# The last seven steps of a packed graph convolution in another order, and a ninth gathered tile fetched by rows

## The chip, the cores and the metric

The kernel runs on one core of a Trainium2 chip. Its time is the device time of one execution in microseconds (us); lower is better. The engines of the core are TensorE (PE in the profile), VectorE (DVE), ScalarE (ACT), GpSimd (POOL) and SyncE (SP). Each has a program of its own that it works off in order; they wait for one another through semaphores.

## The reference

One layer of a message-passing network over 12500 nodes of 128 features and 400000 edges that are sorted by destination:

```python
rbf = jnp.exp(-(distances[:, None] - centers) ** 2 / (2.0 * width * width))      # 50 centres
cut = 0.5 * (jnp.cos(jnp.pi * distances / CUTOFF) + 1.0) * (distances <= CUTOFF)
W = (jax.nn.silu(rbf @ fw1 + fb1) @ fw2 + fb2) * cut[:, None]
messages = (h[src] @ pw + pb) * W
agg = jax.ops.segment_sum(messages, dst, num_segments=num_atoms)
h2 = h + (jax.nn.silu(agg @ mw1 + mb1) @ mw2 + mb2)
x = _layernorm(x + h2, axis=-1, eps=1e-05)
```

The lengths are drawn from 0 to some 56 and the cutoff is 10, so under a fifth of the edges has a weight other than zero.

## The kernel before

**Tiles.** The kernel packs the edges that are within the cutoff into a dense list while it runs, in seven chunks, and works on the list in tiles of 512 edges (4 groups of 128; `QE = QT * P`). For this input 139 tiles are used (`NL = 139`, numbered `q` = 0 to 138). `proj`, the product h @ pw + pb of all nodes, is first computed and written to memory; a tile then fetches the 512 rows of `proj` that its edges' sources name.

**One tile.** `fetch(q)` lets GpSimd issue one indirect DMA for each group of 128 rows: four for a tile, in order of `q` (line 1088). Two tiles at a time (`o`, an "oct"), `basis` has ScalarE compute the radial basis by a Square and an Exp (lines 1140 and 1144), `first` multiplies it on TensorE (line 1156), and `silu` applies Silu on ScalarE (line 1162). For one tile, `second` multiplies by the second weight matrix into a bank of PSUM (lines 1171 and 1174), `message` multiplies that bank by the gathered rows on VectorE (line 1189), `place` makes the 0/1 matrix of destinations times the cutoff weight on VectorE (line 1201), `sum_up` sums the messages by destination with four matmuls for each window (line 1221), and `add` adds the sums to the table `aggT` on VectorE, at a base read from the packed list (line 1255).

**Tiles fetched by rows.** In twelve tiles the first group of 128 rows isn't gathered by GpSimd. For the eight of `BY_SP` SyncE issues 128 DMAs of one row (512 bytes) each (`one_row`, line 1064), for the four of `BY_ACT` ScalarE does. SyncE reads the row numbers into registers, 32 at a time (line 1060), and writes into one of three buffers in turn. How many rows go into a step is set by a clock that the program keeps while it is written out: `one_by_one` puts rows until `row_at` has passed the clock, and each row counts `A_ROW` = 0.58. The multiplication of that group waits for all 128 rows of the tile (line 1186).

**Nodes.** When all edges up to a node are summed, blocks of nodes are finished: `node_first` (line 1268, then Silu on ScalarE into `zs`, line 1270), `node_second` (line 350), `node_stats` (the residual sum, line 1305, and the layernorm's statistics, line 1309), `deviations` (small VectorE operations, lines 1316 to 1319, then a Sqrt on ScalarE, line 1325), `scales` (lines 1335 and 1336), `normalize` (line 1356 on ScalarE or 1353 on VectorE) and a store from SyncE (line 193). The first 80 blocks of 128 nodes go four at a time, and their deviations sixteen blocks at a time (16 columns); the last are named in `TAIL`: 80 and 84 of four blocks, 88, 90, 92, 94 and 96 of two. ScalarE loads another table whenever it goes from Exp to Silu, to Sqrt and back (ACT_TABLE_LOAD in the profile).

**What sets the order.** All of it stands in the program as it is written. A loop over `q` in `range(NL - 7)` has the steps of tiles 0 to 131; the last seven steps (132 to 138) and the end are written out one by one, since each has other node blocks beside it. Each engine takes its instructions in this order, so what stands ahead on an engine delays what stands behind it. SyncE's queue holds loads of `x`, stores of the output and the row DMAs in one order; a store there waits until ScalarE has normalized its block. In addition, the gathers of tiles below `UPTO` = 90 depend on a VectorE instruction some places back (`BACK`, `behind`, `logged`, and the dependence added in `fetch`). `keep_busy(n)` issues n matmuls whose results nobody reads.

Of the kernel before, what the change touches and what calls it, by code (L numbers as in the profile page):

```python
# [43 lines left out]
NL = 139  # L44
# [16 lines left out]
BACK = ((0, 66), (16, 38), (26, 46), (39, 38), (52, 26), (63, 19), (88, 46), (102, 14),  # L61
        (111, 8))
UPTO = 90
VECTORS = ("TensorScalarPtr", "TensorTensor", "CopyPredicated", "TensorReduce", "TensorCopy",
           "BNStats")
# [28 lines left out]
def kernel(  # L94
# [346 lines left out]

    vectors = []

    def logged(i):

        if i.engine == mybir.EngineType.DVE and str(i.opcode) in VECTORS:
            vectors.append(i.name)

    nc.push_inst_callback(logged)

    def behind(q):

        return next(n for at, n in reversed(BACK) if q >= at)

# [627 lines left out]
    def fetch(q, idx=None, table=None, js=range(QT)):  # L1082
        got = quad_sb[place_of(q) if q >= 0 else 0]
        for j in js:
# [3 lines left out]
            g = nc.gpsimd.indirect_dma_start(  # L1088
                out=got[:, j, :], out_offset=None, in_=proj if table is None else table,
                in_offset=bass.IndirectOffsetOnAxis(ap=i, axis=0))  # L1090
# [312 lines left out]
    def nodes(q):  # L1403
# [6 lines left out]
        for k, t0 in enumerate(early):  # L1410
            if begin[t0][0] - 5 == q:
                load_x(t0)
            if begin[t0][2] == q:
# [3 lines left out]
                if k % 4 == 3:  # L1417
# [9 lines left out]
    st_of, deep = {}, []  # L1427

    def tail(q):

        for k, t0, step in ((9, 80, node_first), (8, 80, node_second), (8, 84, node_first)):
# [142 lines left out]
    for q in range(NL - 7):  # L1574
# [72 lines left out]
    assert not todo and counted and not ready and len(deep) == 1 and done[0] == NL - 7  # L1647
# [12 lines left out]
    st = statistics()  # L1660
    node_stats(80, st)
# [16 lines left out]
    sum_up(q, message(q))  # L1678
    second(q + 2)
    node_second(88)  # L1680
    place(q + 1)
    add(q)
    normal(1)
# [183 lines left out]
```

## Time and profile before

| | |
|---|---|
| runs | 720.64, 720.64 and 723.32 us, median 720.64 us |
| profiled execution | 718.53 us, of which the span is 717.0 us |
| granted TensorE clock, mean | 0.918 |
| GpSimd indirect DMAs | 551, from 6.78 to 701.36 us of the span |
| busy share of the span | TensorE 82%, VectorE 78%, GpSimd 74%, ScalarE 56% |
| last matmul of `sum_up` | starts at 707.73 us |
| end of the last normalization on VectorE | 713.24 us |

All times in the profile count from the start of the span; the execution is 1.5 us longer than it. A row of the timeline gives the start, the duration, the engine, the line, the operation, what it writes and reads, and in brackets how long the engine had been idle before it and what ended the idle time. Busy shares are means over 717 us and over stages with different limits; they don't say which engine the others wait for.

### The profile page before, as it was taken

The page shows a single profiled execution, that of the slowest core. Times are in us where ns is not written, and L with a number is a line of the kernel's source. Part 1 is how long each engine was busy: PE and PEld are TensorE (multiplying, and loading weights), DVE is VectorE, ACT ScalarE, POOL GpSimd, SP SyncE. Part 2 cuts the span into 40 slices and gives each one's busy share as a digit, 9 for nine tenths or more (in the row PEclk, how much of TensorE's full clock was granted, in tenths as well). Part 3 has the DMA queues.
Part 4 walks back from the last instruction along what each step waited for, and adds up shares of the span by engine and source line. Part 5 has one row for each costly group of instructions (what it writes and reads, how often), then busy time and mean ns, then how long its engine had stood idle before and what let it go on. Part 6 is the DMA issues. An engine that isn't in the chain of part 4 may idle for free.

```text
span 717.0 us, 14503 instructions
## 1 busy us (share of the span) xinstructions
PE 584.6 (82%) x3526; PEld 461.1 (64%) x3526; DVE 561.7 (78%) x1741; ACT 401.7 (56%) x569; POOL 529.2 (74%) x565
## 2 busy tenths in 40 slices
PE   5878868688898788697878997799998887878775
PEld 5767557566676576575666765577686654665554
DVE  8899899759998799989979994876856545555765
ACT  6557625245645667554645566466765843574564
POOL 6777777777777777777777777777777777777771
PEclk9998787899999899889987999699999998999997
DMA  8996533333334333443344334444543444344242
GB/s 259 328 328 206 161 99 102 98 102 84 115 103 130 83 87 100 118 126 85 87 113 118 99 116 116 130 131 120 153 113 91 138 111 114 101 142 126 56 131 79
DMA packets 54004, 91.41 MB, mean 127 GB/s; under 512 B 14272, under 2 KB 21536, under 8 KB 53914
## 3 DMA queue, kind: packets, MB, share of 16 engines
q0 software_dynamic: 17712, 36.51, 20.4%
q1 hardware_dynamic: 24916, 35.61, 15.0%
q10 hardware_dynamic: 11286, 18.31, 8.0%
q8 instruction: 29, 0.48, 0.3%
q14 instruction: 61, 0.50, 0.2%
HBM read 74.59 MB, written 15.79 MB: 126 GB/s over the span
## 4 chain that ended last, share of the span: by engine, by line
POOL 18%; DVE 15%; DMA 13%; issue 13%; PE 9%; ACT 3%; ACTq 3%; DVEq 1%; SPq 0%; POOLq 0%
POOL quad L1088 14%; DMA quad<-proj,srci 8%; POOL x L1088 3%; DVE hot L1201 3%; PE ph L1156 3%; DMA x<-proj,srci 3%; DVE msg L1189 2%; ACTq L1064 2%; PE sums L1221 2%; PE bank L1174 1%; DVE aggT L1255 1%; DMA packed<-line,at_i 1%; DVE quad L1189 1%; DMA pair<-packed 1%; DVE quad L1201 1%
## 5 line engine op out<-in xcount | busy, mean ns | idle before, releaser
L1088 POOL DMA_INDIRECT quad<-proj,srci x402 | 381.7, 950 | 122.6 <-issue 97.3
L1174 PEld LDWEIGHTS bank<-fw_sb,s 128*128 128x128 f32 x1112 | 158.1, 205 | 60.3 <-issue 50.2
L1174 PE MATMUL bank<-fw_sb,s 128*128 128x128 f32 x1112 | 158.2, 289 | 0.0
L1156 PE MATMUL ph<-rbf,w_sb 102*128 102x512 f32 x278 | 143.7, 642 | 12.3 <-ACT s L1162 8.3
L1221 PEld LDWEIGHTS sums<-hot,msg 128*128 128x128 f32 x816 | 109.2, 200 | 53.4 <-issue 26.0
L1162 ACT ACTIVATE s<-ph 128x1024 f32<-128x1024 f32 x70 | 71.2, 1017 | 122.3 <-PE ph L1156 121.9
L1201 DVE TENSOR_SCALAR hot<-iota_n,dl,cut 128x80 f32<-128x80 f32 (+4 forms) x408 | 111.1, 347 | 22.9 <-PE sums L1221 20.9
L1221 PE MATMUL sums<-hot,msg 128*128 128x80 f32 (+4 forms) x816 | 111.5, 282 | 15.4 <-DVE msg L1189 15.2
L1088 POOL DMA_INDIRECT x<-proj,srci x94 | 90.0, 958 | 28.7 <-issue 22.3
L1171 PE MATMUL bank<-fb_b,ones_b 96*128 96x512 bf16 x139 | 56.0, 403 | 42.2 <-DVE msg L1189 22.0
L1189 DVE TENSOR_TENSOR msg<-bank,quad 128x512 f32<-128x512 f32 (+1 forms) x78 | 52.5, 673 | 41.1 <-DMA quad<-proj,srci 34.5
L1156 PEld LDWEIGHTS ph<-rbf,w_sb 102*128 102x128 f32 x278 | 51.2, 205 | 51.7 <-issue 37.3
L1255 DVE TENSOR_TENSOR aggT<-aggT,sums 128x80 f32 (+4 forms) x209 | 54.1, 259 | 30.7 <-PE sums L1221 12.4
L1140 ACT ACTIVATE rbf<-d_sb,rbf_bias,rbf_scale 102x512 f32<-102x512 f32 x70 | 56.2, 803 | 8.0 <-issue 8.0
L1088 POOL DMA_INDIRECT quad<-in_x_dram,srci x48 | 47.5, 990 | 15.9 <-issue 12.5
L1162 ACT ACT_TABLE_LOAD x34 | 43.6, 1283 | 15.3 <-issue 14.9
L1144 ACT ACT_TABLE_LOAD x35 | 44.9, 1283 | 11.4 <-issue 9.6
L1221 PE MATMUL sums<-quad,quad 128*128 128x128 f32 (+3 forms) x296 | 41.8, 285 | 11.0 <-DVE quad L1189 11.0
L350 PEld LDWEIGHTS bank<-pw_sb,xT 128*128 128x128 f32 (+1 forms) x292 | 42.3, 209 | 11.2 <-issue 5.6
L1144 ACT ACTIVATE rbf<-rbf 102x512 f32<-102x512 f32 x70 | 44.1, 630 | 7.9 <-issue 5.6
L1221 PEld LDWEIGHTS sums<-quad,quad 128*128 128x128 f32 x296 | 38.6, 201 | 12.7 <-DVE quad L1189 12.4
L350 PE MATMUL bank<-pw_sb,xT 128*128 128x128 f32 (+1 forms) x292 | 42.8, 293 | 0.8 <-ACT xT L995 0.6
(281 smaller groups left out, 796.9 us busy)
## 6 DMA issues: line engine op xcount, KB each, us to landing
d_sb<-near_d ACTq DMA_DIRECT2D x67, 256.0 KB
row_sb<-proj SPq DMA_DIRECT2D x1024, 0.5 KB
x<-in_x_dram SPq DMA_DIRECT2D x46, 256.0 KB
row_sb<-proj ACTq DMA_DIRECT2D x512, 0.5 KB
quad<-proj,srci POOLq DMA_INDIRECT x402
proj<-hp SPq DMA_DIRECT2D x24, 256.0 KB
out_dram<-x SPq DMA_DIRECT2D x22, 256.0 KB
x<-proj,srci POOLq DMA_INDIRECT x94
```

Of the source, the lines that this page charges most:

```text
L350: nc.tensor.matmul(to[:m, k, :], lT[:, k * P:k * P + m], w, start=False, stop=(k == a + c - 1))
L1088: g = nc.gpsimd.indirect_dma_start(out=got[:, j, :], out_offset=None, in_=proj if table is None else table, in_offset=bass.IndirectOffsetO ...
L1140: a = nc.scalar.activation(rbf[:u], d[:u], AF.Square, bias=rbf_bias[:u], scale=rbf_scale[:u])
L1144: nc.scalar.activation(rbf[:u], rbf[:u], AF.Exp, scale=-1.0 / (2.0 * width * width))
L1156: nc.tensor.matmul(ph[:, h, :], w1_sb[:2 * KR, h, :], rbf[:2 * KR], start=True, stop=True)
L1162: nc.scalar.activation(s[:, :n], ph[:, :n], AF.Silu)
L1171: nc.tensor.matmul(pu, ones_b[:, :P], bias_b["fb2"].rearrange("k j f -> k (j f)"), start=True, stop=False)
L1174: nc.tensor.matmul(pu[:, j * H:(j + 1) * H], s[:, j * P:(j + 1) * P], fw2_sb, start=False, stop=(j == QT - 1))
L1189: nc.vector.tensor_mul(msg[:, a:b, :], pu_of[q].rearrange("p (j f) -> p j f", j=QT)[:, a:b, :], got_of[q][:, a:b, :])
L1201: nc.vector.tensor_scalar(hot[:, j, :wide(q)], iota_n[:, :wide(q)], dl[:, at[0], at[1]], cut[:, at[0], at[1]], op0=OP.is_equal, op1=OP.mult)
L1221: nc.tensor.matmul(pa[:, k * W:k * W + wide(q)], msg[:, j, :], hot[:, j, :wide(q)], start=(j % n == 0), stop=(j % n == n - 1))
L1255: nc.vector.tensor_add(to, to, pa[:, k * W:k * W + wide(q)])
```

## The change

**The gathers.** `BACK`, `UPTO`, `VECTORS`, `logged`, `behind` and the dependence that `fetch` added are gone, so no gather of a tile depends any longer on a place in VectorE's program. Those dependences that the data need stay.

**The rows.** `BY_SP` has nine tiles in place of eight: 118 and 133 are replaced by 113, 124 and 135. GpSimd issues 550 indirect DMAs in place of 551, SyncE 128 row DMAs and four register loads more. Once no chunk is left to be packed (`todo` is empty), a row counts `A_ROW_LATE` = 0.42 in place of 0.58, so more rows stand in a step. On SyncE's queue the part from the store of block 60 to the store of block 64 was, before (`row_sb` is the buffer of rows; `x_87` holds block 64, the other `x_` blocks after it):

```order
L193 DMA out_dram<-x_86 128x512
L1064 DMA row_sb<-proj 1x512 x9
L193 DMA x_91<-in_x_dram 128x512
L1064 DMA row_sb<-proj 1x512 x9
L193 DMA x_92<-in_x_dram 128x512
L1064 DMA row_sb<-proj 1x512 x9
L193 DMA x_93<-in_x_dram 128x256
L1064 DMA row_sb<-proj 1x512 x2
L193 DMA x_86<-in_x_dram 128x256
L193 DMA out_dram<-x_87 128x512
```

The same part of SyncE's queue now, and one row group further:

```order
L189 DMA out_dram<-x_86 128x512
L1047 DMA row_sb<-proj 1x512 x12
L189 DMA x_91<-in_x_dram 128x512
L1047 DMA row_sb<-proj 1x512 x12
L189 DMA x_92<-in_x_dram 128x512
L1047 DMA row_sb<-proj 1x512 x4
L1043 TENSOR_LOAD at_row
L1047 DMA row_sb<-proj 1x512 x8
L189 DMA x_93<-in_x_dram 128x256
L1047 DMA row_sb<-proj 1x512 x13
L189 DMA out_dram<-x_87 128x512
L189 DMA x_86<-in_x_dram 128x256
L1047 DMA row_sb<-proj 1x512 x11
```

Twelve rows stand in a step where nine stood, and the last eleven rows (of tile 135) stand behind the store of block 64, where before all rows of tile 133 stood ahead of it.

**The node blocks.** The statistics of block 76 move from the loop to `tail(NL - 9)`, and the deviations of 64, 68 and 72 are computed without it, earlier, in the loop; so `scales`, the normalizations and the stores of these three blocks come earlier too, two of them ahead of the last octs' bases. Block 76 goes into the group of 80, 84, 88 and 90 (16 columns in place of 12). The two last octs' `basis` moves from step 131 to step 132, and their `first` and `silu` to the steps 133 and 134. On ScalarE the twelve instructions from the Silu of tiles 134 and 135 on were, before (`s` is the Silu of an oct, `zs` of a node block, `dev` the Sqrt, `rbf` a basis):

```order
L1162 ACTIVATE s<-ph 128x1024
L1270 ACTIVATE zs<-bank_170 128x512
L1325 ACT_TABLE_LOAD
L1325 ACTIVATE dev<-v,eps 128x16
L1140 ACTIVATE rbf<-d_sb,rbf_bias,rbf_scale 102x512
L1144 ACT_TABLE_LOAD
L1144 ACTIVATE rbf<-rbf 102x512
L1140 ACTIVATE rbf<-d_sb,rbf_bias,rbf_scale 102x512
L1144 ACTIVATE rbf<-rbf 102x512
L1270 ACT_TABLE_LOAD
L1270 ACTIVATE zs<-bank_168 128x512
L1162 ACTIVATE s<-ph 128x1024
```

On ScalarE now, from the Silu of that same oct:

```order
L1141 ACTIVATE s<-ph 128x1024
L1335 ACTIVATE x_87<-x_87,by,rs 128x128 x4
L1249 ACTIVATE zs<-bank_170 128x512
L1335 ACTIVATE x_88<-x_88,by,rs 128x128 x4
L1249 ACTIVATE zs<-bank_169 128x512
L1119 ACTIVATE rbf<-d_sb,rbf_bias,rbf_scale 102x512
L1123 ACT_TABLE_LOAD
L1123 ACTIVATE rbf<-rbf 102x512
L1119 ACTIVATE rbf<-d_sb,rbf_bias,rbf_scale 102x512
L1123 ACTIVATE rbf<-rbf 102x512
L1335 ACTIVATE x_89<-x_89,by,rs 128x128 x4
L1141 ACT_TABLE_LOAD
```

The Sqrt with its table no longer stands between two Silus of node blocks here, and both these Silus come ahead of the bases.

**The last steps.** In each of them `second(q + 2)` now stands ahead of `sum_up(q)`, node work is in other places, and `keep_busy` has 3 + 2 + 2 matmuls in place of 1 + 1. On TensorE the steps of tiles 136 and 137 were, before (`hot_1075,msg_1080` is the sum of tile 136, `hot_1192,msg_680` that of 137, line 1174 the `second` of tile 138, line 1288 the residual of block 96, line 1268 `node_first` of block 92):

```order
L1221 MATMUL sums<-hot_1075,msg_1080 128x128 x4
L1171 LDWEIGHTS ones_b
L1171 MATMUL bank_169<-fb_b,ones_b 128x512
L1174 MATMUL bank_169<-fw_sb,s 128x128 x4
L1285 LDWEIGHTS ones_b
L1285 MATMUL bank_167<-mb_b,ones_b 128x256
L1288 MATMUL bank_167<-x_89,ident 128x128 x2
L1288 MATMUL bank_167<-x_89,ident 84x128 x2
L1267 LDWEIGHTS mb_b
L1267 MATMUL bank_170<-ones_b,mb_b 128x256
L1268 MATMUL bank_170<-aggT,mw_sb 128x256
L1221 MATMUL sums<-hot_1192,msg_680 128x128 x4
```

On TensorE now, from the `second` of tile 138 to the `node_first` of block 92:

```order
L1153 MATMUL bank_170<-fw_sb,s 128x128 x4
L1264 LDWEIGHTS ones_b
L1264 MATMUL bank_168<-mb_b,ones_b 128x256
L1267 MATMUL bank_168<-x_89,ident 128x128 x2
L1267 MATMUL bank_168<-x_89,ident 84x128 x2
L1200 MATMUL sums<-hot_1075,msg_1080 128x128 x4
L1246 LDWEIGHTS mb_b
L1246 MATMUL bank_167<-ones_b,mb_b 128x256
L1247 MATMUL bank_167<-aggT,mw_sb 128x256
```

The `second` of tile 138 and the residual of block 96 stood behind the sum of tile 136 and stand ahead of it now; what remains between the sums of 136 and 137 is the node work of block 92 and the three `keep_busy` matmuls. The diff:

```diff
-BACK = ((0, 66), (16, 38), (26, 46), (39, 38), (52, 26), (63, 19), (88, 46), (102, 14),
-        (111, 8))
-UPTO = 90
...
-BY_SP = (22, 45, 62, 67, 86, 102, 118, 133)
+BY_SP = (22, 45, 62, 67, 86, 102, 113, 124, 135)
...
+A_ROW_LATE = 0.42
...
     def one_by_one():
         row_at[0] = max(row_at[0], clock[0] - 8.0)
         while singles[0] and row_at[0] < clock[0]:
-            row_at[0] += A_ROW
+            row_at[0] += A_ROW if todo else A_ROW_LATE
             one_row(0)
...
-            g = nc.gpsimd.indirect_dma_start(
+            nc.gpsimd.indirect_dma_start(
                 out=got[:, j, :], out_offset=None, in_=proj if table is None else table,
                 in_offset=bass.IndirectOffsetOnAxis(ap=i, axis=0))
-            if 0 <= q < UPTO and len(vectors) > behind(q):
-                tc.add_manual_dep(
-                    g.ins, vectors[-1 - behind(q)],
-                    mybir.DependencyInfo(mybir.DependencyClass.Sync, mybir.DependencyReason.DATA))
...
-            if begin[t0][2] == q:
+            if begin[t0][2] == q and t0 != early[-1]:
                 if k % 4 == 0:
                     st_of[0] = statistics()
                 node_stats(t0, st_of[0][:, k % 4 * 4:])
-                if k % 4 == 3:
+                if k % 4 == 3 or t0 == early[-2]:
                     deep.append(deviations(early[k // 4 * 4:k + 1], st_of[0]))
...
     def tail(q):
+        if q == NL - 9:
+            last_st.append(statistics())
+            node_stats(early[-1], last_st[0])
...
             for o in (q // 4 * 2 + 4, q // 4 * 2 + 5):
-                if 2 * o < NL:
+                if 2 * o < NL and q < NL - 8:
                     basis(o)
...
     q = NL - 7
     house(q)
-    sum_up(q, message(q))
+    msg = message(q)
     second(q + 2)
+    sum_up(q, msg)
+    node_second(84)
+    node_stats(80, last_st[:, 4:])
     bases_of(list(range(q, NL)))
     place(q + 1)
-    scales(*deep.pop(0))
+    for o in (octs(q), octs(q + 1)):
+        basis(o)
     add(q)
-    first(octs(q))
-    silu(octs(q))
-    node_second(84)
     normal(1)
-    st = statistics()
-    node_stats(80, st)
...
     q += 1
     house(q)
-    sum_up(q, message(q))
+    msg = message(q)
     second(q + 2)
-    first(octs(q))
-    silu(octs(q))
-    normal(1)
+    first(octs(q - 1))
+    silu(octs(q - 1))
+    sum_up(q, msg)
     place(q + 1)
+    node_stats(84, last_st[:, 8:])
     add(q)
     node_first(88)
-    node_stats(84, st[:, 4:])
...
-    dev = deviations([80, 84, 88, 90], st)
+    dev = deviations([76, 80, 84, 88, 90], last_st)
...
     p, q = NL - 2, NL - 1
     house(p)
-    sum_up(p, message(p))
+    msg = message(p)
     node_second(92)
+    keep_busy(3)
+    sum_up(p, msg)
+    node_stats(92, st)
     sum_up(q, message(q, (0, 1)), (0,))
     add(p)
     node_first(94)
+    sum_up(q, message(q, (1, 2)), (1,))
     normal(1)
-    sum_up(q, message(q, (1, 2)), (1,))
-    node_stats(92, st)
     add(q, (0,))
+    keep_busy(2)
     sum_up(q, message(q, (2, 3)), (2,))
-    normal(2)
+    normalize(*ready.pop(0), on=(0, 1))
+    store()
+    normal(1)
     node_second(94)
-    keep_busy(1)
     sum_up(q, message(q, (3, 4)), (3,))
     add(q, (1,))
     node_first(96)
     node_stats(94, st[:, 2:])
+    keep_busy(2)
     dev = variances([92, 94], st)
-    keep_busy(1)
```

More of the change, by code (lines that the diff above doesn't have):

```diff
@@ L440, in before_it @@
         return max((m for m in range(q) if place_of(m) == place_of(q)), default=-1)
[L442 to L453, printed above, removed]
     def room(q):
@@ L1425, in nodes @@
                 load_x(t0)
-    st_of, deep = {}, []
+    st_of, deep, last_st = {}, [], []
     def tail(q):
+        if q == NL - 9:
+            last_st.append(statistics())
+            node_stats(early[-1], last_st[0])
         for k, t0, step in ((9, 80, node_first), (8, 80, node_second), (8, 84, node_first)):
@@ L1677 @@
     house(q)
-    sum_up(q, message(q))
+    msg = message(q)
     second(q + 2)
+    first(octs(q - 1))
+    silu(octs(q - 1))
+    sum_up(q, msg)
     node_second(88)
@@ L1682 @@
     add(q)
-    normal(1)
     node_first(90)
-    node_stats(88, st[:, 8:])
+    node_stats(88, last_st[:, 12:])
     load_x(94)
-    normal(1)
     q += 1
     house(q)
-    sum_up(q, message(q))
+    msg = message(q)
     second(q + 2)
     node_second(90)
+    sum_up(q, msg)
     place(q + 1)
+    node_stats(90, last_st[:, 14:])
+    dev = deviations([76, 80, 84, 88, 90], last_st)
+    silu_next()
     add(q)
     load_x(96)
-    node_stats(90, st[:, 10:])
-    dev = deviations([80, 84, 88, 90], st)
-    silu_next()
     q += 1
     house(q)
-    sum_up(q, message(q))
+    msg = message(q)
     second(q + 2)
+    node_x(96)
+    sum_up(q, msg)
     place(q + 1)
-    node_x(96)
     st = statistics()
+    scales(*dev)
     add(q)
     node_first(92)
-    scales(*dev)
-    normal(1)
+    normal(2)
     place(q + 2)
@@ L1753 @@
     store()
-    nc.remove_inst_callback(logged)
     def more(q):
```

5 lines of the change are left out of this document (2 added, 3 removed).

## The prediction

> **What bounds the kernel now.** I read GpSimd's waits first, then its timeline's ends:
>
> ```profile
> span 717.0 us, 14503 instructions
> POOL quad L1088 <- issue: 109.8, 360, 0.3
> POOL quad L1088 <- DVE aggT L1255: 2.4, 8, 0.3
> POOL quad L1088 <- DVE hot L1201: 1.5, 5, 0.3
> 6.78 1.21 POOL L1088 DMA_INDIRECT quad<-in_x_dram,srci  x1 [1.60 <-DVE srci L566]
> 691.68 0.94 POOL L1088 DMA_INDIRECT quad<-proj,srci  x1 [0.30 <-DVE x L1305]
> 692.93 0.96 POOL L1088 DMA_INDIRECT quad<-proj,srci  x1 [0.30 <-issue]
> 699.18 0.94 POOL L1088 DMA_INDIRECT quad<-proj,srci  x1 [0.30 <-issue]
> 700.42 0.94 POOL L1088 DMA_INDIRECT quad<-proj,srci  x1 [0.30 <-issue]
> ```
>
> The waits' columns are total, count and longest. GpSimd's pauses are 0.3 us whether the profile finds a releaser or not, so none is a wait: a gather starts each 1.24 to 1.25 us (699.18 to 700.42), from 6.78 to 700.42 us. GpSimd's stream of gathers sets the time up to there. The rest is what follows the last gather: 717.0 − 700.42 = 16.6 us. The chain of waits gives what a gather needs to land (its start, its length; eight such rows between 600 and 685 us lie between these two), and VectorE's and TensorE's timelines show who uses the data:
>
> ```profile
> 644.16 2.45 DMA quad<-proj,srci
> 652.90 4.10 DMA quad<-proj,srci
> 667.90 2.50 DMA quad<-proj,srci
> 670.53 0.69 DVE L1189 TENSOR_TENSOR quad<-bank,quad 128x512 f32<-128x512 f32 x1 [0.85 <-DMA quad<-proj,srci]
> 697.34 0.69 DVE L1189 TENSOR_TENSOR msg<-bank,quad 128x512 f32<-128x512 f32 x1
> 706.29 0.48 DVE L1189 TENSOR_TENSOR quad<-bank,quad 128x128 f32<-128x128 f32 x2
> 706.63 0.49 PE L1221 MATMUL sums<-quad,quad 128*128 128x128 f32 x2 [0.58 <-DVE quad L1189]
> 707.73 0.38 PE L1221 MATMUL sums<-quad,quad 128*128 128x128 f32 x2
> 712.65 0.59 DVE L1353 TENSOR_SCALAR x<-x,rs,by 128x128 f32<-128x128 f32 x2
> ```
>
> At 670.53 a message still waits for its data. The last gather (700.42) should land by 702.9 at 2.50, but its message is in the pair at 706.29, so some 3.6 us late: at the very end the gathers don't bound, the chain of compute behind them does. Where it fell behind is seen on ScalarE and TensorE, and in the windows of TensorE's clock:
>
> ```profile
> 664.85 1.02 ACT L1162 ACTIVATE s<-ph 128x1024 f32<-128x1024 f32 x1 [3.78 <-PE ph L1156]
> 670.89 0.60 ACT L1270 ACTIVATE zs<-bank 128x512 f32<-128x512 f32 x1 [5.03 <-PE bank L1268]
> 671.51 1.28 ACT L1325 ACT_TABLE_LOAD   x1
> 679.07 0.60 ACT L1270 ACTIVATE zs<-bank 128x512 f32<-128x512 f32 x1
> 679.72 0.38 PE L1171 MATMUL bank<-fb_b,ones_b 96*128 96x512 bf16 x1 [2.32 <-ACT zs L1270]
> 698.09 1.31 PE L1221 MATMUL sums<-hot,msg 128*128 128x128 f32 x8 [2.39 <-DVE msg L1189]
> 689.38 1.05 PE L1174 MATMUL bank<-fw_sb,s 128*128 128x128 f32 x8
> 699.62 1.92 PE L1174 MATMUL bank<-fw_sb,s 128*128 128x128 f32 x8
> 692.13:695.54 3.41, 2.67 (x22) 2.58 (x22) 2.38 (x7) 2.65 (x5) 2.50 (x4) 1.00 0.69 212
> 695.54:698.95 3.41, 1.02 (x9) 0.87 (x8) 3.08 (x12) 1.59 (x2) 2.72 (x3) 1.00 0.36 92
> 698.95:702.37 3.42, 3.42 (x17) 3.21 (x16) 2.97 (x12) 0.20 (x1) 1.88 (x2) 0.50 0.23 56
> ```
>
> (A window's columns: length, then busy time of TensorE, its weight loads, VectorE, ScalarE and GpSimd, then the granted clock.) Between 671.51 and 679.07 ScalarE loads tables, takes the Sqrt and computes two bases ahead of a `zs` for which TensorE waits 2.32 us. Later TensorE idles 2.39 us for the message of tile 136, its window 695.54 to 698.95 has 1.02 us of work, and in the next one the clock is 0.50: the `second` of tile 138 takes 1.92 us in place of 1.05. The sums of 137 and 138 stand behind that.
>
> **The change part by part.**
>
> *One gather fewer.* One interval of 1.25 us less, since nothing else holds GpSimd: the last gather starts at 699.17. The bounds are 0 and 1.25; I take 1.25, because every interval quoted has that length. −1.25.
>
> *No dependence on VectorE.* GpSimd never waited for it (longest pause 0.3), so 0; the cover is that the gathers are issued late in any case, and GpSimd still waits for the buffers that the data need. What would be late without that cover is only an earlier gather, which would gain.
>
> *The ninth row tile.* SyncE's own price:
>
> ```profile
> L1060 SPq TENSOR_LOAD <-at_row x32: 2120/2164/3061, 76.7 to 643.9; - x32
> 562.97 5.75 SPq L1064 DMA_DIRECT2D row_sb<-proj  x18
> L1064 SPq DMA_DIRECT2D row_sb<-proj x128: 227/228/350, 521.7 to 586.6; - x128
> 606.86 0.28 DVE L1186 TENSOR_TENSOR quad<-bank,row_sb 128x128 f32<-128x128 f32 x1
> ```
>
> A row costs 5.75 / 18 = 0.32 us, a load of 32 registers 2.16, so a tile 128 × 0.32 + 4 × 2.16 = 49.6 us of SyncE at least. Before, the 128 rows of tile 118 took 64.9 us (521.7 to 586.6), at nine in a step; at twelve in a step that is 64.9 × 9/12 = 48.7, under SyncE's own 49.6. With the loads and stores between I take 52 us a tile: tile 113 done at 521.7 + 52 = 573.7, 124 at 625.7, 135 at 677.7. Needed: tile 118's rows were multiplied at 606.86; five tiles earlier at 20 gathers × 1.25, and one gather less, is 580.6 for 113; eleven tiles on, at 43 gathers, 634.4 for 124; 42 more, 686.9 for 135 (a tile by ScalarE lies between). So each is 7 to 9 us early, and the 1152 rows and the extra register loads cost 0. The eleven last rows now stand behind the store of block 64, which waits for its normalization behind the Silu that is at 664.85: about 664.85 + 1.02 + 1.6, then 11 × 0.32, some 671 us. No one waits there.
>
> *The node blocks and bases.* The Sqrt of 64 to 72 and the table loads around it (2 × 1.28 + 0.31) move ahead of a Silu at which ScalarE had been idle 3.78 and 5.03 us: covered there, 0 on the path. Gone is the stretch of 7.6 us in which it stood ahead of two `zs`. The one thing later is the `first` and `silu` of the last octs, by one step of 5 us: tile 136's Silu now ends one step ahead of its `second`, in place of two. Its own work (two matmul pairs and a Silu of 1.02) fits into a step, so 0, at least while the bases start on time.
>
> *The last steps.* Their rows on TensorE, and ScalarE's last normalizations:
>
> ```profile
> 701.54 1.45 PE L1288 MATMUL bank<-x,ident 128*128 128x128 f32 x8
> 706.95 0.27 PE L347 MATMUL bank<-mb_b,ones_b 96*128 96x256 bf16 x1
> 707.07 0.61 PE L350 MATMUL bank<-mw_sb,zs 128*128 128x128 f32 x4
> 707.51 0.38 PE L1439 MATMUL ph<-mb_b,ones_b 96*128 96x512 bf16 x1
> 706.20 3.17 ACT L1356 ACTIVATE x<-x,by,rs 128x128 f32<-128x128 f32 x8
> ```
>
> `second` of tile 138 and the residual of block 96 come ahead of the sum of 136, in the very gap of 2.39 us. They cost 1.05 + 0.38 and, of the residual's 1.45 at half clock, some 1 us of TensorE there, hidden by the wait for the message; and the window that had 1.02 us of work then has about 3, so I expect no 0.50 after it. The five more `keep_busy` matmuls are 0.38 us each in waits. If the messages wait for nothing but data, the end is: landing 2.50; 0.34 from the last message to its sum (706.29 to 706.63); and from the last sum to VectorE's end 713.24 − 707.73 = 5.51. That is 8.35 us from the last gather's start, against 713.24 − 700.42 = 12.82 before. At the slowest landing, 4.10, it is 9.95. Between the last two sums TensorE still has the `second` of block 94. It takes 0.73 us (706.95 to 707.68), and its `zs` stands on ScalarE behind normalizations; I put 0.45 of it on the path, so 8.8 us, nearer to the lower end because the row of 2.50 is the last one of this stage. That is −4.0. The 3.76 us from VectorE's end to the span's end are stores and stay. A gain beyond is possible: eight normalizations (3.17 us, to 709.37) stood directly ahead of the last Silu and now a part of them is on VectorE; worth 0.3 at most, left out of the sum.
>
> [...]
>
> *Sum.* 717.0 − 1.25 − 4.0 = 711.7 for the span. The profiled execution was 718.53, 1.5 over its span and 2.1 under the runs' median of 720.64; I take the same difference of −5.3 off the median: 715.4.
>
> **The rivals.** About 0.5%, 3.6 us, is what a measurement of this kernel can tell from no change.
>
> *A: only the gather counts.* `second(q + 2)` ahead of each sum costs TensorE 0.38 + 1.05 with overlaps, about 1.1 us, in each step. If the message is there first, the sum and everything behind waits that long, and the lag of 3.6 us stays. For it: the message of 136 at 697.34 wasn't waiting for data. Against it: TensorE idled 2.39 us right then. 720.64 − 1.25 = 719.4.
>
> *B: the rows come late (slower).* If SyncE's pace doesn't rise as the order has it, tile 135's multiplication waits, and with it VectorE and every sum behind it. It decides from (686.9 − 521.7) / 3 = 55.1 us a tile on; at 58 tile 135 is done at 695.7, 8.8 us late, against the 5.3 gained: 724.1. For it: 64.9 us before, and a queue in which stores wait:
>
> ```profile
> SPq L193 <- ACT x L1356: 84.8, 14, 26.6
> ```
>
> One such wait of 26.6 us ahead of a row tile would be enough. Against it: the stores of the blocks concerned come earlier.
>
> *C: the clock falls again.* Another window in the last 20 us with too little TensorE work. At half clock a full window loses up to 1.7 us (half of 3.42); I take 1.5: 716.9. Against it: seven `keep_busy` matmuls and the `second` in the gap.
>
> [...]
>
> **How the numbers follow.** Forecast 0.65, A 0.15, B 0.06, C 0.12, D 0.02. The forecast's own range is 714.4 to 717.0: landing up to 4.10 adds 1.6, the normalizations on VectorE take off 0.3, and 0.7 are for TensorE's queue. The whole range reaches down to 712.8, if the median falls on the profiled execution (718.53 − 5.3 = 713.2), and up to 718.9, which holds C and a third of A. Faster by over 0.5% (under 717.0) is the forecast but 0.02 and half of C, 0.69; the same is A, the rest of C and those 0.02, 0.23; slower is B and D, 0.08.
>
> **What would show it.** Right: 550 gathers with pauses of 0.3, the last at about 699.2; VectorE's multiplications of row tiles 113, 124 and 135 without a wait; the messages of tiles 134 to 138 waiting for the gather's DMA rather than for TensorE; no window at clock 0.50 after 688; VectorE's last normalization some 8.8 us behind the last gather. Wrong: an idle of VectorE ahead of a row multiplication (B), messages of 138 again over 3 us behind their data (A), a `second` of 1.9 us (C), gathers over 1.3 us apart (D).

## The result and the profile after

The changed kernel takes 715.74 us (median of 6 runs, 713.59 to 716.95), the kernel before 721.4 us (6 runs beside it, 720.64 to 723.32). The ratio is 0.9919 with a 95% interval of 0.99 to 0.9938, so 5.8 us less, between 4.5 and 7.2. The forecast was 715.4 us in a range of 712.8 to 718.9. The span of the profiled execution fell from 717.0 to 712.1 us.

GpSimd's waits and its last gathers in the changed kernel:

```profile
span 712.1 us, 14771 instructions
POOL quad L1071 <- issue: 108.6, 356, 0.3
692.23 0.94 POOL L1071 DMA_INDIRECT quad<-proj,srci  x1 [0.30 <-DVE x L1284]
699.73 0.95 POOL L1071 DMA_INDIRECT quad<-proj,srci  x1 [0.30 <-issue]
```

Ahead of a gather behind the first one no pause is over 0.3 us, and the last of 550 indirect DMAs (seven of them write the packed list) starts at 699.73, which is 0.69 us earlier than the last of 551 before. What VectorE and TensorE do with the last tiles (line 1168 is the message, 1165 its part that uses rows, 1200 the sums, 1332 a normalization; the row at 684.03 belongs to tile 134, whose rows ScalarE fetches):

```profile
680.40 0.69 DVE L1168 TENSOR_TENSOR msg<-bank,quad 128x512 f32<-128x512 f32 x1 [1.12 <-DMA quad<-proj,srci]
684.03 0.28 DVE L1165 TENSOR_TENSOR quad<-bank,row_sb 128x128 f32<-128x128 f32 x1
689.32 0.29 DVE L1165 TENSOR_TENSOR quad<-bank,row_sb 128x128 f32<-128x128 f32 x1
693.52 0.68 DVE L1168 TENSOR_TENSOR msg<-bank,quad 128x512 f32<-128x512 f32 x1
702.34 0.29 DVE L1168 TENSOR_TENSOR quad<-bank,quad 128x128 f32<-128x128 f32 x1
707.72 0.59 DVE L1332 TENSOR_SCALAR x<-x,rs,by 128x128 f32<-128x128 f32 x2
692.38 1.05 PE L1153 MATMUL bank<-fw_sb,s 128*128 128x128 f32 x8
694.27 1.16 PE L1200 MATMUL sums<-hot,msg 128*128 128x128 f32 x8
702.83 0.39 PE L1200 MATMUL sums<-quad,quad 128*128 128x128 f32 x2
```

The message of tile 136 comes at 693.52 (697.34 before). TensorE doesn't idle ahead of its sum, which follows the `second` of tile 138 at 1.05 us (1.92 before). The last message is at 702.34, 2.6 us after the start of its gather. The prediction had named one sign of being right that isn't here: no message from tile 134 on has a wait for the gather's DMA in its row. The last such wait is that of tile 133 (680.40). VectorE ends at 708.31: 8.58 us behind the last gather, where it was 12.82. From there to the span's end it is 3.79 us (3.76 before). So of the 4.9 us by which the two profiled spans differ, 0.69 are the gathers and 4.24 the last steps. TensorE's windows follow, with the columns of the prediction. In this trace the granted clock falls sixteen times, from 45.89 to 708.08, at times that are whole multiples of 3.413 us apart, and these lie elsewhere in this execution than in that of the kernel before; the windows are counted back from its fall at 708.08, behind the last matmul:

```profile
694.43:697.84 3.41, 2.16 (x16) 1.57 (x16) 3.34 (x14) 1.25 (x5) 2.50 (x3) 1.00 0.20 56
697.84:701.25 3.41, 3.05 (x23) 2.42 (x22) 2.00 (x8) 2.70 (x8) 2.23 (x3) 1.00 0.36 118
701.25:704.67 3.42, 2.97 (x18) 1.62 (x15) 2.58 (x12) 3.04 (x8) 0.00 (x0) 1.00 0.51 172
```

No window is at clock 0.50 from 688 up to the last sum. On ScalarE the two Silus of node blocks now stand ahead of the bases, as the order showed:

```profile
670.82 0.60 ACT L1249 ACTIVATE zs<-bank 128x512 f32<-128x512 f32 x1 [2.78 <-PE bank L1247]
675.22 0.60 ACT L1249 ACTIVATE zs<-bank 128x512 f32<-128x512 f32 x1 [2.25 <-PE bank L1247]
675.71 0.81 ACT L1119 ACTIVATE rbf<-d_sb,rbf_bias,rbf_scale 102x512 f32<-102x512 f32 x1
```

The second of them ends at 675.8 where it ended at 679.7, since it waits for TensorE now and not for a table.

### The profile page after: what moved, and what is told of

It reads as the page before. It is cut to its first block, busy times and chain, and to the rows that moved or that the text cites. A ratio compares the mean times of both kernels' runs of the same rounds, so it can differ in the third digit from the quotient of the medians.

```text
span 712.1 us, 14771 instructions
## 1 busy us (share of the span) xinstructions
PE 584.0 (82%) x3531; PEld 459.7 (65%) x3531; DVE 560.3 (79%) x1744; ACT 403.2 (57%) x568; POOL 528.6 (74%) x564
## 3 DMA queue, kind: packets, MB, share of 16 engines
q10 hardware_dynamic: 11286, 18.31, 7.7%
## 4 chain that ended last, share of the span: by engine, by line
DVE 21%; POOL 17%; DMA 15%; issue 14%; PE 13%; ACT 3%; ACTq 3%; SPq 2%; DVEq 2%; POOLq 0%
POOL quad L1071 16%; DMA quad<-proj,srci 11%; DVE hot L1180 5%; PE ph L1135 5%; DVE msg L1168 3%; PE sums L1200 2%; ACTq L1047 2%; PE bank L1153 2%; DMA pair<-packed 2%; DVE bank L518 2%; DVE aggT L1234 1%; POOL x L1071 1%; DVE r_d L512 1%; DVE nodes L522 1%; DMA x<-proj,srci 1%
## 5 line engine op out<-in xcount | busy, mean ns | idle before, releaser
L1153 PEld LDWEIGHTS bank<-fw_sb,s 128*128 128x128 f32 x1112 | 156.9, 204 | 55.5 <-issue 46.6
L1200 PEld LDWEIGHTS sums<-hot,msg 128*128 128x128 f32 x816 | 110.3, 201 | 55.6 <-issue 26.3
L1180 DVE TENSOR_SCALAR hot<-iota_n,dl,cut 128x80 f32<-128x80 f32 (+4 forms) x408 | 109.4, 343 | 19.3 <-PE sums L1200 17.6
```

Of the source, the lines that this page charges most:

```text
L1153: nc.tensor.matmul(pu[:, j * H:(j + 1) * H], s[:, j * P:(j + 1) * P], fw2_sb, start=False, stop=(j == QT - 1))
L1180: nc.vector.tensor_scalar(hot[:, j, :wide(q)], iota_n[:, :wide(q)], dl[:, at[0], at[1]], cut[:, at[0], at[1]], op0=OP.is_equal, op1=OP.mult)
L1200: nc.tensor.matmul(pa[:, k * W:k * W + wide(q)], msg[:, j, :], hot[:, j, :wide(q)], start=(j % n == 0), stop=(j % n == n - 1))
```

## The experiments

The first four run the three parts of the change alone, and one piece of the third. The table gives the ratio to the kernel before (from several runs of each, beside it on the same chip), and from one profiled execution the span, the start of the last gather and the distance from there to the end of VectorE's work. The first four kernels behind the changed one were measured on one chip, the next four on another; differences in us are worked out from the ratio.

| kernel | ratio, 95% interval | span | last gather | distance |
|---|---|---|---|---|
| before | | 717.0 | 700.42 | 12.82 |
| changed | 0.9919, 0.99 to 0.9938 | 712.1 | 699.73 | 8.58 |
| rows alone | 0.9986, 0.9968 to 1.0003 | 717.6 | 700.05 | 13.60 |
| blocks and last steps alone | 0.9949, 0.9929 to 0.9968 | 716.4 | 702.02 | 10.72 |
| dependence alone | 0.9997, 0.9984 to 1.001 | 720.0 | 703.59 | 12.82 |
| `second` first alone | 1.0015, 0.9998 to 1.0032 | 721.3 | 702.04 | 15.71 |
| changed, sum first | 0.9995, 0.9973 to 1.0017 | 717.6 | 700.64 | 13.27 |
| changed, less `keep_busy` | 0.9931, 0.9906 to 0.9956 | 715.0 | 699.73 | 11.71 |
| before, gap filled | 0.9989, 0.9968 to 1.001 | 714.9 | 699.56 | 11.68 |
| changed, tile 131 | 1.0108, 1.0077 to 1.0139 | 724.2 | 698.18 | 21.90 |

**Rows alone.** Nine row tiles and the denser rows, in the kernel before.

```diff
-BY_SP = (22, 45, 62, 67, 86, 102, 118, 133)
+BY_SP = (22, 45, 62, 67, 86, 102, 113, 124, 135)
+A_ROW_LATE = 0.42
...
-            row_at[0] += A_ROW
+            row_at[0] += A_ROW if todo else A_ROW_LATE
```

> The kernel before with the nine row tiles and the denser rows alone. By the theory that the gathers set the time up to the last steps and that these then take as long as before: the last gather starts 0.7 to 1.25 us earlier than in the kernel before (699.2 to 699.7 against 700.42), VectorE's end still lies 12.8 us behind it, the span falls by 0.7 to 1.25 us (715.7 to 716.3 against 717.0). By the rival that the last steps are bound by their compute alone, the time is that of the kernel before, and the distance grows to 13.5 to 14 us. By the rival of late rows, VectorE waits ahead of a row multiplication, and the time grows.

By the ratio 1.0 us less (2.3 less to 0.2 more): what one gather is worth, but the interval also holds nothing. No multiplication of a row tile waited for its rows. The profiled execution has a longer end, 13.60 us, which is what the theory of last steps bound by their compute alone had expected; the run doesn't decide between the two. One reason for the longer end is in two windows of TensorE's clock:

```profile
677.50:680.91 3.41, 1.12 (x10) 1.09 (x10) 3.31 (x14) 2.21 (x3) 2.79 (x3) 1.00 0.39 100
680.91:684.32 3.41, 3.41 (x7) 1.15 (x6) 1.42 (x5) 0.00 (x0) 2.50 (x4) 0.50 0.23 55
```

Here it is the gap behind ScalarE's stretch, at 677 to 680, that left 1.12 us of work in a window, and the clock was half in the next; in the profiled execution of the kernel before that gap did no such harm, and the one at 696 to 698 did. Which gap halves the clock differs between executions.

**Blocks and last steps alone.** The kernel before with the regrouped node blocks, the moved bases and the last seven steps of the changed kernel, with its own rows and dependence.

```diff
-            if begin[t0][2] == q:
+            if begin[t0][2] == q and t0 != early[-1]:
...
-                if 2 * o < NL:
+                if 2 * o < NL and q < NL - 8:
...
-    sum_up(q, message(q))
+    msg = message(q)
     second(q + 2)
+    sum_up(q, msg)
+    node_second(84)
...
```

> The kernel before with the new order of node blocks, bases and last steps alone. Theory: the last gather stays at 700.4, and VectorE's end comes 8.6 us behind it in place of 12.8, so the span is 712.8, 4.2 us less. Rival that the order gains only together with the other parts: a distance over 10 us, and less than 2.5 us gained.

3.7 us less by the ratio (2.3 to 5.1), near the 4.2 expected. The profiled execution has a distance of 10.72 in place of 8.6, for another reason than the order: its last message waited for data.

```profile
703.75 0.29 DVE L1189 TENSOR_TENSOR quad<-bank,quad 128x128 f32<-128x128 f32 x1 [0.20 <-DMA quad<-proj,srci]
706.34 0.29 DVE L1189 TENSOR_TENSOR quad<-bank,quad 128x128 f32<-128x128 f32 x1 [1.79 <-DMA quad<-proj,srci]
```

The last gather started at 702.02, so its data took 4.3 us, against at most 2.6 in the changed kernel. With the order changed, the end can be bound by the data again, as the prediction had it, and how long the last data take varies.

**Dependence alone.** The kernel before without `BACK` and what belongs to it.

```diff
-            g = nc.gpsimd.indirect_dma_start(
+            nc.gpsimd.indirect_dma_start(
...
-            if 0 <= q < UPTO and len(vectors) > behind(q):
-                tc.add_manual_dep(
...
```

> The kernel before without the gathers' dependence on VectorE alone. Theory: no change (within 0.5 us of 717.0 in the span; single gathers differ, their sum doesn't). Rival of stretched gathers: more gathers over 1.28 us apart than the 53 of the kernel before, and over 1 us more in all.

0.2 us less by the ratio (1.2 less to 0.7 more): nothing. The span of the profiled execution is longer, with the last gather at 703.59. Of that, 2.4 us are one pause:

```profile
134.57 0.25 DVE L903 CAST srci<-bank 128x88 int32<-128x88 f32 x1 [0.51 <-PE bank L896]
135.10 0.94 POOL L1070 DMA_INDIRECT quad<-proj,srci  x1 [2.66 <-DVE at_row L919]
```

The gather follows VectorE's writing of the row numbers (`srci`) by 0.3 us. That is a dependence the data need; read so, the gathers had caught up with the packing there in this execution. The ratio doesn't show that it happens as a rule. Both signs of the rival did appear in this one profile, 64 gathers over 1.28 us apart and the last one 3.17 us later, but the other profiles speak against it: in the five with the dependence there are 52 to 61 such gathers (mean 55.6), in the five without it 47 to 64 (mean 55).

**`second` first alone.** The kernel before, with the `second` of tile q + 2 (and the residual of block 96) ahead of the sum of tile q.

```diff
-    sum_up(q, message(q))
+    msg = message(q)
     second(q + 2)
+    sum_up(q, msg)
...
     second(q + 2)
+    node_x(96)
+    sum_up(q, msg)
     place(q + 1)
-    node_x(96)
```

> The kernel before, with the second of tile q + 2 ahead of the sum of tile q in steps 132 to 136, and the residual of block 96 too, and nothing else. If filling the gap of 2.39 us ahead of the sum of tile 136 is what brings the gain: no window at clock 0.50 after 695, the second of tile 138 takes 1.05 us, the distance from the last gather to VectorE's end is 10.5 to 11.3 us, and 1.5 to 2.3 us are gained. If the stretch of 7.6 us on ScalarE alone is the cause: the distance stays over 12.3. If everything is the order: 8.6 to 9.

None of the three: the distance grew to 15.71, and the ratio says 1.1 us more (0.1 less to 2.3 more). TensorE's timeline shows why:

```profile
676.91 1.12 PE L1268 MATMUL bank<-aggT,mw_sb 128*128 128x512 f32 x2 [0.71 <-DVE aggT L1255]
681.30 0.59 PE L1171 MATMUL bank<-fb_b,ones_b 96*128 96x512 bf16 x1 [3.26 <-ACT zs L1270]
681.68 1.91 PE L1174 MATMUL bank<-fw_sb,s 128*128 128x128 f32 x8
683.38 1.91 PE L1221 MATMUL sums<-hot,msg 128*128 128x128 f32 x8
```

The `second` needs a bank that ScalarE's Silu of a node block has still to read, and that Silu stood at the end of the stretch with the tables and bases. Before, the sum of tile 132 ran ahead of this wait (676.30); now it stands behind it, at 683.38, and at half clock. So this piece by itself puts a sum behind ScalarE's lateness.

**Changed, sum first.** The reverse: the changed kernel with the sum ahead of `second` again in five steps, all else kept.

```diff
-    msg = message(q)
+    sum_up(q, message(q))
     second(q + 2)
-    sum_up(q, msg)
     node_second(84)
...
-    msg = message(q)
+    sum_up(q, message(q))
     second(q + 2)
     node_x(96)
-    sum_up(q, msg)
     place(q + 1)
```

> The changed kernel with the sum of tile q ahead of the second of tile q + 2 again in the steps 132 to 136. If the gain of the last steps comes from the node blocks and bases on ScalarE (the order of second alone, in the run before this, gained nothing): the time of the changed kernel within 1 us, distance from the last gather to VectorE's end 8.5 to 9.5 us. If both are needed: TensorE idles 1.5 to 2.5 us ahead of the sum of 136 again, a distance over 10.5 us, and at least 2 us slower than the changed kernel.

The whole gain is gone (0.9995), though ScalarE has the new order. TensorE waits for messages with its other work queued behind the sums (the first row is VectorE's part of the message of tile 134):

```profile
684.82 0.28 DVE L1165 TENSOR_TENSOR quad<-bank,row_sb 128x128 f32<-128x128 f32 x1
681.90 1.16 PE L1200 MATMUL sums<-hot,msg 128*128 128x128 f32 x8 [1.92 <-DVE msg L1168]
683.11 1.71 PE L1153 MATMUL bank<-fw_sb,s 128*128 128x128 f32 x8
698.80 1.16 PE L1200 MATMUL sums<-hot,msg 128*128 128x128 f32 x8 [2.84 <-DVE msg L1168]
700.02 1.05 PE L1153 MATMUL bank<-fw_sb,s 128*128 128x128 f32 x8
```

Up to tile 134 this run is as early as the changed kernel: 684.82 is 15.82 us ahead of its last gather, where the changed kernel has 15.70 and the kernel before 13.64. Behind it the lead is lost, to the two waits shown and to a window at half clock from 683.33 on, in which the `second` takes 1.71 us; how much each of them cost isn't separated. With the run before this one: neither piece gains in the end without the other. The order on ScalarE frees the bank in time, and only then can `second` fill TensorE's wait for the message. The bank's part in it is in the changed kernel's trace, where the `second` behind the last large `zs` waits 0.69 us for it, not 3.26:

```profile
675.87 0.38 PE L1150 MATMUL bank<-fb_b,ones_b 96*128 96x512 bf16 x1 [0.69 <-ACT zs L1249]
```

Which of the other moves of the third part (node work in other places, a normalization on VectorE) is needed beside these wasn't tried.

**Changed, less `keep_busy`.**

```diff
     node_second(92)
-    keep_busy(3)
     sum_up(p, msg)
...
-    keep_busy(2)
     sum_up(q, message(q, (2, 3)), (2,))
```

> The changed kernel without the three matmuls ahead of the sum of 137 and the two ahead of the third sum of 138; the two at the end stay. If TensorE's clock hangs on the work in a window: the window that holds 697 to 698.7 has 0.4 to 0.5 of its length in work in place of 0.63, the next one is at half clock in those executions in which the windows lie as in the profile of the changed kernel, and the time grows by 0 to 1.5 us. Rival, that only the gap's length counts (no gap over 2 us is left): no window at half clock, no change.

By the ratio 5.0 us faster than before (3.2 to 6.8), so the difference from the changed kernel isn't resolved. The windows don't lie as in the changed kernel's profile here, so the first theory can't be judged at 697: the two around it, from 693.81 and from 697.22, had 2.42 and 2.89 us of work, and the clock didn't fall there. It fell later, though no gap of TensorE was over 2 us, so the rival, that only a gap's length counts, doesn't fit. That was when the last data of this execution took 4.5 us and TensorE had nothing to do:

```profile
704.22 0.29 DVE L1168 TENSOR_TENSOR quad<-bank,quad 128x128 f32<-128x128 f32 x1 [2.10 <-DMA quad<-proj,srci]
704.56 0.80 PE L1200 MATMUL sums<-quad,quad 128*128 128x128 f32 x2 [1.85 <-DVE quad L1168]
700.63:704.04 3.41, 1.33 (x10) 0.94 (x8) 1.09 (x4) 2.68 (x7) 0.04 (x1) 1.00 0.49 165
704.04:707.46 3.42, 2.70 (x8) 1.49 (x8) 2.06 (x10) 0.53 (x2) 0.00 (x0) 0.50 0.32 110
```

Whether the five matmuls would have kept the clock through that wait can't be read from one execution.

**Before, gap filled.** Six matmuls that nobody reads, in the gap of 2.39 us.

```diff
+    keep_busy(6)
     sum_up(q, message(q))
     second(q + 2)
     place(q + 1)
     node_x(96)
```

> The kernel before with six matmuls that nobody reads ahead of the sum of tile 136, where TensorE idled 2.39 us, and nothing else. If the half clock after that gap cost the last steps: no window at 0.50 after 698, the second of tile 138 takes 1.05 us, the distance from the last gather to VectorE's end falls from 12.8 to 11.1 to 12.0, the time by 0.8 to 1.7 us. If the message's lateness sets the end whatever TensorE's clock: no change in the distance.

```profile
694.88 1.46 PE L1439 MATMUL ph<-mb_b,ones_b 96*128 96x512 bf16 x6
697.43 1.16 PE L1221 MATMUL sums<-hot,msg 128*128 128x128 f32 x8 [1.09 <-DVE msg L1189]
698.64 1.05 PE L1174 MATMUL bank<-fw_sb,s 128*128 128x128 f32 x8
694.53:697.95 3.42, 2.33 (x15) 1.35 (x14) 2.73 (x11) 1.25 (x2) 2.77 (x3) 1.00 0.35 92
697.95:701.36 3.41, 3.39 (x28) 2.93 (x26) 3.24 (x14) 0.62 (x3) 1.95 (x3) 1.00 0.21 52
```

The profile does what the theory says: full clock, 1.05 us, and a distance of 11.68, which is 1.14 less. Without the six matmuls the first of the two windows would have had about 1.0 us of work in place of 2.33 (an estimate: their 1.46 us, less what overlaps the matmuls ahead of them). The ratio gives 0.8 us less, 2.3 less to 0.7 more: the right size, not resolved. By the profiles, the half clock was about a quarter of what the last steps lost (1.14 of 4.24).

**Changed, tile 131.** The price of rows that come late: the rows of the last tile are wanted four tiles earlier.

```diff
-BY_SP = (22, 45, 62, 67, 86, 102, 113, 124, 135)
+BY_SP = (22, 45, 62, 67, 86, 102, 113, 124, 131)
```

> The changed kernel with tile 131 in place of 135 as the last row tile, so that its rows are wanted 20 us earlier at the same pace of SyncE. If the pace of 50 to 55 us a tile holds: the rows are there at 678 to 682 and wanted at about 669, VectorE waits 8 to 12 us ahead of tile 131's row multiplication, and 3 to 9 us of it are left at the end, since the steps behind it have some 1 us each to catch up: 716 to 721 in the span. If SyncE can put rows faster when it isn't held by the order: no wait and the time of the changed kernel.

```profile
680.95 0.29 DVE L1165 TENSOR_TENSOR quad<-bank,row_sb 128x128 f32<-128x128 f32 x1 [9.84 <-DMA row_sb<-proj]
681.30 2.11 PE L1200 MATMUL sums<-quad,quad 128*128 128x128 f32 x8 [9.48 <-DVE quad L1165]
695.80 0.28 DVE L1165 TENSOR_TENSOR quad<-bank,row_sb 128x128 f32<-128x128 f32 x1
714.09 0.28 DVE L1168 TENSOR_TENSOR quad<-bank,quad 128x128 f32<-128x128 f32 x1
```

VectorE waits 9.84 us, as worked out, but none of it is caught up: the span is 12.1 us longer than the changed kernel's, more than I expected. Part of the surplus is a second price of the wait: TensorE idled 9.48 us in it, the clock was half from 677.06 to 687.30, and the sum behind it took 2.11 us in place of 1.16. The rest of this trace shows the pace of the last steps by themselves. The gathers are far ahead (the last one starts at 698.18, its message is at 714.09), and from the row multiplication of tile 134 to the last message it takes 18.29 us (695.80 to 714.09). In the changed kernel it takes 18.31 (684.03 to 702.34). So in the changed kernel, too, these steps go at the pace of their own compute, and the last data come just in time; there is no slack to make up for a late input.

**A tenth row tile, a fifth by ScalarE, and both.** Three tries at a faster kernel, with the changed kernel beside them.

```diff
-BY_SP = (22, 45, 62, 67, 86, 102, 113, 124, 135)
-BY_ACT = (36, 68, 100, 134)
+BY_SP = (22, 45, 62, 67, 80, 92, 103, 114, 125, 136)
+BY_ACT = (30, 56, 82, 108, 134)
...
-A_ROW = 0.58
-A_ROW_LATE = 0.42
+A_ROW = 0.45
+A_ROW_LATE = 0.40
...
-HIDE = (3, 2, 4)
+HIDE = (3, 3, 5)
```

The first try has the lines on `BY_SP` and `A_ROW`, the second those on `BY_ACT` and `HIDE`, the third all of them; the fourth kernel is the changed one.

> The changed kernel with ten tiles whose first group SyncE fetches by rows (22, 45, 62, 67, 80, 92, 103, 114, 125, 136), put into the steps more densely (0.45 and 0.40). If the gathers still set the time up to the last steps and SyncE keeps up: 549 gathers, no wait of VectorE for rows, 1.25 us less than the changed kernel (0 to 2 with what single gathers vary). If SyncE is at its end: VectorE waits for rows, as in the run with tile 131, and the kernel is slower by about the longest such wait.

> The changed kernel with five tiles whose first group ScalarE fetches by rows (30, 56, 82, 108, 134) in place of four, eleven rows for each two tiles in place of nine. If ScalarE's idle time hides 128 more DMA issues: 549 gathers, 1.25 us less than the changed kernel. If they delay a Silu that TensorE waits for: 0 or slower.

> Both of these: 548 gathers, 2.5 us less than the changed kernel if both hold.

> The changed kernel once more beside these, for comparison on the same chip: 0.992 of the kernel before, 0.990 to 0.994.

These four ran on a third chip, on which every kernel took half as long again: the kernel before 1065.33 us (9 runs, 1058.0 to 1072.68), the changed one 1113.78, the tries 1146.72, 1120.76 and 1153.21 us. There the changed kernel is slower than the one before, 1.0443 (1.0387 to 1.0499). In the trace of the changed kernel there, engines stand still without a releaser far longer than in its trace above, and the mean granted TensorE clock is 0.764 against 0.921. Four rows of the waits and one of SyncE's timeline there, and then the first of these rows in the trace above:

```profile
PEld bank L1153 <- issue: 150.7, 78, 17.0
POOL quad L1071 <- DVE msg L1168: 123.9, 23, 17.6
DVE msg L1165 <- DMA row_sb<-proj: 38.0, 2, 20.3
DVE quad L1165 <- DMA row_sb<-proj: 5.7, 1, 5.7
899.28 20.45 SPq L1047 DMA_DIRECT2D row_sb<-proj  x29
```

```profile
PEld bank L1153 <- issue: 46.6, 44, 3.4
```

In the stretch at 899.28 SyncE takes 0.71 us for a row (20.45 / 29, a load of registers among them; 54.9 / 128 = 0.43 for the last tile of the trace above), VectorE waits 43.7 us for rows in three tiles, and GpSimd waits for VectorE. That is near the 48 us by which the changed kernel is slower there, and it would be rival B, but there is no trace of the kernel before on that chip to compare with. And the try with ten row tiles waits only 3.3 us for rows, in two tiles,

```profile
DVE quad L1165 <- DMA row_sb<-proj: 2.4, 1, 2.4
DVE msg L1165 <- DMA row_sb<-proj: 0.9, 1, 0.9
```

and is slower still, so late rows don't explain the order of the four. Why that chip's engines stand still isn't settled, nor why the changed kernel loses there; what one row tile more would bring on chips like those of the other runs stays open.

## Why the prediction was right

**One gather: −1.25.** The profiled executions gave −0.69, the rows alone −1.0 by the ratio, in an interval that holds 0. The size can't be read from one pair, since the start of the last gather varies: over five profiled kernels with 551 gathers it lies at 699.56 to 703.59 us (mean 701.5), over five with 550 at 698.18 to 700.64 (mean 699.7). The cause holds: no pause over 0.3 us ahead of a gather behind the first in the changed kernel.

**No dependence: 0.** Right: 0.9997. The one long pause in its profile is a wait for row numbers (2.66 us ahead of the gather at 135.10), and gathers over 1.28 us apart are as many with the dependence as without it (means 55.6 and 55). So D's sign, gathers over 1.3 us apart, doesn't set the two kernels apart either.

**Row tile: 0.** Right, and by the terms of the sum. The last tile's rows in the changed kernel, and SyncE's register loads:

```profile
L1047 SPq DMA_DIRECT2D row_sb<-proj x128: 227/228/403, 627.1 to 682.0; - x128
L1043 SPq TENSOR_LOAD <-at_row x12: 2155/2179/2237, 516.1 to 667.6; - x12
```

54.9 us for a tile where 52 were taken, done at 682.0 where 677.7 was, and wanted at 689.32 where 686.9 was worked out: 7.3 us early. At the point from which rival B decides, 55.1 us a tile, there was thus less room than 52 let it seem. The eleven rows behind the store of block 64 were put at 671; they were issued from 678.78 on, since SyncE was busy up to then, with the rows ahead of that store (issued at 677.11) and a load. The run with tile 131 shows that rows late by 9.84 us cost all of it and more; on the slow chip rows did come late.

**Node blocks: 0 on the path; last steps: −4.0.** The sum was right (−4.24 in the profiles, −3.7 alone), its division was not. I put the gain on `second` in the gap and the end of the half clock, and let the node blocks count nothing themselves. The row of tile 134 in the kernel before shows where the gain arises:

```profile
686.78 0.28 DVE L1186 TENSOR_TENSOR quad<-bank,row_sb 128x128 f32<-128x128 f32 x1
```

It is 13.64 us ahead of the last gather; in the changed kernel (684.03) it is 15.70. So 2.06 of the 4.24 us are gained before the gap of tile 136 is reached, 2.15 from there to the last sum, and 0.03 behind it. In all five profiles with the old order of node blocks and bases this lead is at most 13.64 us, in the four with the new one, the run with the sum first among them, 15.70 to 16.45 (the run with tile 131 is left out, since its rows came late). The step that failed is therefore the 0 for the node blocks: ScalarE's stretch, for which TensorE waited 2.32 us, was on the path, and the lead that its removal brings is about half of the gain. The runs also show that neither part keeps its gain without the other: `second` first without the node blocks loses (15.71 us of distance), the node blocks without `second` first gain nothing in the end (13.27). The half clock alone, when the gap is filled, is 1.14 of the 4.24 us.

The distance of 8.58 came by the terms in number: 2.6 to the last message (2.50 taken), 0.49 to its sum (0.34), 5.48 from the sum to VectorE's end (5.51). The `second` of block 94, for which 0.45 had been allowed, ran right ahead of that sum and is what the 0.15 are from: some 0.3 less than I had put on the path. That the 2.6 came so near to the landing of 2.50 is in part luck. The last messages didn't wait for data; they came at the pace of the steps' own compute, as the run with tile 131 shows (18.29 us against 18.31), and that pace happens to end where the data of this execution were there. In two other executions the last data took 4.3 and 4.5 us and did set the end.

**Rival A** is refuted as stated and right in its place: `second` ahead of a sum does cost, where the bank it needs is late (3.26 us of waiting, in the run with `second` first alone). **Rival C** stayed out in the profile of the changed kernel, but the run with less `keep_busy` fell to half clock when the last data were late, so it isn't excluded in other executions. In the last steps as they were before, the clock was half somewhere in each of the three profiles: from 698.95 on in the kernel before, from 680.91 with the rows alone, from 701.71 with the dependence alone.

In each of the two traces of the kernel before and of the changed kernel the granted clock falls only at times that are whole multiples of 3.413 us apart (nineteen falls from 53.83 to 712.60 before, sixteen from 45.89 to 708.08 now), and where they lie differs between executions (698.95 in the kernel before, 683.33 in the run with the sum first, which differ by 4.6 windows). In the run with the sum first a gap of 2.84 us ahead of 698.80 lay across two windows, left 2.39 and 1.60 us of work in them, and was followed by full clock (1.05 us at 700.02); a gap of 1.92 us left 1.49 us in its window and was followed by half clock (1.71 us at 683.11). So the prediction was right to go by the work in the window: in the last steps a window was followed by half clock with 1.02 us of work in the kernel before, 1.12 with the rows alone, 1.33 with less `keep_busy` and 1.49 with the sum first, and of the two gaps of that run it was the shorter one. Where the boundary lies isn't settled: after 1.60 us the clock stayed full here, after 1.75 us it fell in the trace of the changed kernel (the window from 544.24 to 547.65).

## What to carry to other kernels

When an engine in order idles for one input, work put ahead of that wait fills it only if the work's own inputs and buffers are there already; find what frees them and move that first, then judge both moves together, since each alone can measure as nothing or as a loss (here 1.0015 for `second` first alone and 0.9995 for all but it, against 0.9919 for all). A stage whose own compute takes as long as its data need to arrive has no slack: a late input there is paid in full, and here with more: 12.1 us for a wait of 9.84, in which TensorE's clock fell to half. And a transfer that lands 7 us early with its issuing engine nearly full is hidden only as long as that engine keeps its speed: at 54.9 us a tile the rows were 7.3 us early, and where SyncE took 0.71 us for a row VectorE waited 43.7 us for them. Before reading a window of the clock, find where the windows begin in that execution (698.95 and 683.33 above were 4.6 windows apart).

## What the runs showed that was not expected

The time the last gather's data took was at most 2.6 us in one execution and 4.3 and 4.5 us in two others of kernels with the same last messages; the bounds taken from the chain of waits, 2.45 to 4.10, were too narrow above. Stores of the output are issued at that time; whether they are the reason wasn't tried. Single gathers and pauses shift the start of the last gather by up to 4 us between profiled executions (699.56 to 703.59 with 551 of them), which is nearly as much as the 4.9 us between the spans before and after. And the verdict on the change depends on the chip: 0.9919 where it was measured first, 1.0443 on a chip on which the engines stood still far longer (150.7 us against 46.6 ahead of the weight loads of `second`).
